# Block comparisons with the turns innermost, a chunk in three more steps, and a fourteenth shared pair ahead of the routed ones

## The chip, the core and the metric

The kernel runs on one core of a Trainium2 chip. The metric is device time in microseconds (us). Three runs of the kernel before took 564.23, 564.28 and 566.93 us; the median is 564.28 us. A run that was profiled took 563.65 us.

## The reference, cut to what matters

The input `x` holds 8 batches of 512 rows of 128 numbers. It is normalised, and causal attention with 16 heads of 8 dimensions and a mixture of experts both read the normalised rows. Their sum is added to `x`.

```
x = L0_attn_x
xn = _layernorm(x, axis=-1)
x = x + _L0_attn_ref(xn, ...) + _L0_ffn_ref(xn, ...)

# _L0_ffn_ref, over T = 4096 rows
shared = _ffn(xf, shared_gate, shared_up, shared_down)     # silu(x @ gw.T) * (x @ uw.T) @ dw.T
probs = jax.nn.softmax(xf @ gate_w.T, axis=-1)
topw, topi = jax.lax.top_k(probs, TOP_K)                   # 2 of 8 experts
topw = topw / (topw.sum(-1, keepdims=True) + 1e-20)
# routed: every row adds its two experts' _ffn, weighted
return (shared + routed).reshape(B, S, H)
```

All experts have 352 hidden units.

## The kernel before, in words

**Attention.** The unit of the loop is a step: scores of two of a group's four heads against some of the keys. A group has five steps (`TILES`: wide, wide, mixed, mixed, half), and with 8 batches of 4 groups there are 160 steps, 0 to 159. In a step PE makes the scores (`fill`, tile scT, L339), ACT takes their exponential (pT, L467), and PE later multiplies pT with the values (`attend`, tile av, L491). Nine steps ahead of that (`AHEAD`) a second set of scores is made (tile sc, L383), whose row maxima DVE takes (`maxima`: diag L417, tops L412, L421 and L422); PE turns the maxima (mT_ps, L439), and SP writes them into the rows of qs (L451), from which the later scores take them.

**Experts beside it.** The rows are worked on in pairs of blocks (256 rows). A pair is three chunks, one for each third of the hidden units. `chunk` multiplies on PE (tile gu, L653), takes a tanh on ACT (L658) and multiplies twice on DVE (th L659, h L661). When a pair's hidden units are there, `down` multiplies once for each of the two blocks (tile y, L684). A shared pair's y is added to `x_sb` by DVE (L695); a routed block's y is scaled by ACT (L691) and scattered by POOL's indirect DMA to `results` in HBM (L668). The list `stream` holds the order: `FIRST` = 13 shared pairs, then 36 routed pairs, then the other three shared pairs. The generator `experts` gives one chunk each time that `extra` is called. It is called before and between the first steps, and then once in each step of the main loop that isn't in the set `alone`: `set(range(3, 21, 2)) | {12, 16, 20}`, so steps 3, 5, 7, 9, 11, 12, 13, 15, 16, 17, 19 and 20 have no chunk. The first routed chunk comes in step 35, the last in step 142, and the last chunk of all in step 151.

**Routing.** `route` is a generator too, and goes on a little in each step. Near its end it finds which row stands at which place of the 72 blocks. Each of 64 turns (32 tiles of 128 rows, two choices) has a block number in `blk` and a position in `pos`. In each of steps 12 to 19 `compare(m)` takes eight turns (`PIECE`): one DVE operation compares all 72 block numbers with the eight (tile what, L1060), and eight DVE operations compare the positions (tile there, L1067). A step later ACT multiplies the comparison with the partition's number into the second half of what (L1074), and another step later `gather_up` makes eight matmuls of 144 columns (tile sums_of, L1079), which DVE adds to found (L1083). In step 20 and 21 DVE also finds the expert of each block (L1091, L1098).

**The end.** When all 72 routed blocks are scattered, POOL issues 16 DMAs that add `results` to `x_sb` (`gather`, L719), for two choices of eight batches. Batches 0 to 5 go first; those of batches 6 and 7, whose rows the last shared pairs still change, are put out after the last chunk. The list gives the batches' order; POOL's own order is the scheduler's. DVE adds the attention's projection (L584), for the last batch behind its adds from POOL, and SP writes the output (L1286) when a batch is complete.

**What sets the order.** The order on PE, DVE, ACT and SP is that in which the Python code issues (`manual_schedule`): in a step the scores, the look ahead, the chunk, the routing's piece, up to two waiting `down`s, then the values. Each of these engines works through its own list in this order. POOL's order is made by the scheduler. Tiles with one buffer (scT, sc) make a step's scores wait for the reader of those before, and gu, y, sums_of and other short tiles share three buffers of PSUM.

Of the kernel before, what the change touches and what calls it, by code (L numbers as in the profile page):

```python
# [10 lines left out]
F32 = mybir.dt.float32  # L11
I32 = mybir.dt.int32
BF16 = mybir.dt.bfloat16
# [12 lines left out]
P = 128  # L26
# [3 lines left out]
NT = B * NC  # L30
# [6 lines left out]
NE = 8  # L37
# [4 lines left out]
NP = TOPK * NT * P  # L42
BLK = P
MB = 2
FIRST = 13
LAST = (13, 14, 15)
PAIR = MB * BLK

# [1 line left out]
NB = (NP // BLK + NE - 1 + MB - 1) // MB * MB  # L50
# [3 lines left out]
PIECE = 8  # L54
# [13 lines left out]
def attn_moe_kernel(  # L68
# [14 lines left out]
    nc = tc.nc  # L83
# [44 lines left out]
    for i in range(NV):  # L128
        t = const.tile([P, NC, H, 32], F32, name=f"v_ext{i}")
# [11 lines left out]
    def constant_rows(t, rows):  # L141
# [11 lines left out]
        base=0, channel_multiplier=1,  # L153
# [14 lines left out]
    for t in v_ext:  # L168
# [10 lines left out]
        base=0, channel_multiplier=-1,  # L179
# [8 lines left out]
        base=0, channel_multiplier=0,  # L188
# [12 lines left out]
    for i in range(2):  # L201
        t = const.tile([P, NF, PAIR], F32, name=f"h{i}")
# [6 lines left out]
        own_p, pattern=[[0, 1]], base=0, channel_multiplier=1, allow_small_or_imprecise_dtypes=True  # L209
# [3 lines left out]
        upto_p, pattern=[[1, P]], base=0, channel_multiplier=0, allow_small_or_imprecise_dtypes=True  # L213
# [24 lines left out]
    def misc(shape, name, dtype=F32):  # L238
        return mi_ps.tile(shape, dtype, tag="mi", name=name)
# [347 lines left out]
    shared = [j for j in range(NT // MB) if j not in LAST] + list(LAST)  # L587
    stream = [("shared", j) for j in shared[:FIRST]]
    stream += [("routed", j) for j in range(NB // MB)]
    stream += [("shared", j) for j in shared[FIRST:]]  # L590
    weights, held, turned, scales = {}, {}, {}, {}
# [188 lines left out]
    hot_pool = early.enter_context(tc.tile_pool(name="hot", bufs=3))  # L780
    ro = early.enter_context(tc.tile_pool(name="router", bufs=1))
# [2 lines left out]
    count = ro.tile([P, PURE + 2 * MIXED], F32, name="count")  # L784
    count16 = ro.tile([P, NB], BF16, name="count16")
    nc.gpsimd.tensor_copy(count16, count_i)
    nc.gpsimd.tensor_copy(count[:, :PURE], count_i[:, : PURE * MB : MB])
    for i in range(2):
        nc.gpsimd.tensor_copy(count[:, ds(PURE + i * MIXED, MIXED)], count_i[:, PURE * MB :])
# [116 lines left out]
    def route():  # L906
# [5 lines left out]
        nc.vector.tensor_reduce(lmax, logits, AX.X, ALU.max)  # L912
        prob = ro.tile([P, NT, NE], F32, name="prob")
        hots = ro.tile([P, TOPK, NT, NE], F32, name="hots")
        equal = ro.tile([P, NT, NE], F32, name="equal")
        nth = ro.tile([P, NT, NE], F32, name="nth")
        left, tops = logits, [lmax]
        for i in range(TOPK):
            if i:
# [47 lines left out]
        nc.vector.reciprocal(psum, psum)  # L967
        total = ro.tile([P, NE], F32, name="total")
        nc.vector.tensor_copy(total, total_ps)
        placed_in = ro.tile([P, NT, NE], F32, name="placed_in")  # L970
        nc.scalar.copy(placed_in, place)
        yield

# [1 line left out]
        over = ro.tile([P, NE, most], F32, tag="rest", name="over")  # L975
# [24 lines left out]
        nc.vector.tensor_tensor(starts, ends, own, ALU.subtract)  # L1000
        apart = ro.tile([P, NE], F32, name="apart")
        paired = ro.tile([P, NE], F32, name="paired")
        where = ro.tile([P, NT, NE], F32, name="where")

        def every(v):
            return v.unsqueeze(1).to_broadcast([P, NT, NE])
# [34 lines left out]
        blk = ro.tile([P, TOPK * NT], BF16, name="blk")  # L1041
# [9 lines left out]
        whats, theres = {}, {}  # L1051

        def compare(m):
            these = ts(m, PIECE)

            def over(v):
                return v[:, these].unsqueeze(2).to_broadcast([P, PIECE, NB])

            what = hot_pool.tile([P, 2, PIECE, NB], BF16, name="what")
            nc.vector.tensor_tensor(  # L1060
                what[:, 0], count16.unsqueeze(1).to_broadcast([P, PIECE, NB]), over(blk),
                ALU.is_equal,
            )
            there = hot_pool.tile([P, PIECE, P], BF16, name="there")
            for t in range(PIECE):
                turn_ = m * PIECE + t
                nc.vector.tensor_scalar(  # L1067
                    there[:, t], upto_p, pos[:, ds(turn_, 1)], float(turn_ + 1),
                    ALU.is_equal, ALU.mult,
                )  # L1070
            whats[m], theres[m] = what, there
# [4 lines left out]
        def gather_up(m):  # L1076
            sums_of = misc([P, 2, NB], "sums_of")
            for t in range(PIECE):
                nc.tensor.matmul(  # L1079
                    sums_of, lhsT=theres[m][:, t], rhs=whats[m][:, :, t], start=(t == 0),  # L1080
                    stop=(t == PIECE - 1),
                )
            nc.vector.tensor_tensor(found, found, sums_of, ALU.add)  # L1083
# [25 lines left out]
        for m in range(pieces + 2):  # L1109
            if m >= 2:  # L1110
                gather_up(m - 2)
            if 1 <= m <= pieces:
                own(m - 1)
            if m < pieces:
                if m % 2 == 0:
                    two = PIECE // NC
                    nc.sync.dma_start(
                        to_table[:, ts(m // 2, two)],
                        rows[:, ts(m // 2, PIECE)].rearrange("p (b c) e -> p b c e", c=NC),
                    )  # L1120
                compare(m)
            else:
                experts_of[m - pieces]()
            yield
# [25 lines left out]
        nc.vector.tensor_scalar(token, number, -float(P), 0.0, ALU.add, ALU.max)  # L1150

    routing = route()
    done_routing = []

# [54 lines left out]
        due(first + (1 if b < 3 else 2), partial(project_qk, b, 1), behind_all)  # L1209
        due(at_ + (8 if b > 1 else 3), partial(project_v, b), behind_all)  # L1210
    routed = -2
    alone = set(range(3, 21, 2)) | {12, 16, 20}
    for t in range(AHEAD):
        while puts:
            puts.pop(0)()
# [131 lines left out]
```

## Time and profile before

| | |
|---|---|
| median of three runs | 564.28 us |
| the profiled execution | 563.65 us |
| its span | 561.5 us |
| PE busy | 530.3 us, 94% |
| DVE busy | 434.9 us, 77% |
| ACT busy | 354.0 us, 63% |
| POOL busy | 261.8 us, 47% |
| comparisons (sums_of, L1079) | 64 matmuls, first at 99.5, last at 127.8 us |
| comparisons (what, L1060) | 8 operations, 748 ns each, 93.1 to 119.7 us |
| first and last start of the adds from `results` (L719) | 523.5 and 552.0 us |

The span is the time between the first and the last instruction on the core; the execution's own time lies 2.15 us above it. A group of the profile gives a source line, an engine, the tile written and those read, the shape, how often it ran, its busy time in total and the mean of one in ns, and behind the second bar the engine's idle time before it and what ended that. A timeline gives the start in us, the time that the merged instructions took and, in brackets, the wait before them. The table of stretches gives the busy time of each engine in it, then the granted TensorE clock as a share of full speed, the busy share of the DMA engines and the GB/s that they moved. PE's matmuls overlap in a pipeline, so what one costs is read from start to start.

### The profile page before, as it was taken

The numbers are of one execution on the slowest core, as the hardware profiler recorded it, in microseconds if no ns is written. First come the engines' busy times: TensorE is split into PE (matmuls) and PEld (weight loads), VectorE is DVE, ScalarE is ACT, GpSimd is POOL, SyncE is SP. The second block draws the span as 40 slices with busy tenths as digits, with TensorE's granted clock in tenths as the row PEclk, the third lists the DMA queues.
The fourth block names the chain that finished last, engine by engine and source line by source line (L and its number), as shares of the span: only waits on it lengthen the run. The fifth ranks groups of instructions, "written<-read, shape, count | busy, mean of one in ns | idle before, by whom it ended". The sixth has DMA issues, their size and how long they took to land.

```text
span 561.5 us, 12501 instructions
## 1 busy us (share of the span) xinstructions
PE 530.3 (94%) x4495; PEld 380.2 (68%) x4495; DVE 434.9 (77%) x1057; ACT 354.0 (63%) x567; POOL 261.8 (47%) x442
## 2 busy tenths in 40 slices
PE   4899988899999999999999999999999999999994
PEld 2676655557675777677776777667776776778762
DVE  5878999999877777877787787778787877877741
ACT  4453444553566766777677776767677766766653
POOL 8630020001342656666556556656655756543630
PEclk9999999989999999999999999999999999999999
DMA  7651353625228583585639585675919586650694
GB/s 216 146 73 24 77 78 97 96 78 103 65 57 130 147 158 107 139 204 129 130 88 154 160 166 138 126 160 137 164 46 198 167 141 200 138 146 4 99 255 100
DMA packets 34114, 70.72 MB, mean 126 GB/s; under 512 B 7028, under 2 KB 9336, under 8 KB 34054
## 3 DMA queue, kind: packets, MB, share of 16 engines
q1 hardware_dynamic: 26278, 56.47, 44.4%
q0 software_dynamic: 6912, 13.20, 12.3%
q8 instruction: 36, 0.59, 0.5%
q10 hardware_dynamic: 864, 0.27, 0.2%
q14 instruction: 24, 0.20, 0.2%
HBM read 52.38 MB, written 17.33 MB: 124 GB/s over the span
## 4 chain that ended last, share of the span: by engine, by line
PE 76%; DVE 17%; ACT 2%; issue 2%; DMA 1%; POOL 0%; DVEq 0%; ACTq 0%
PE gu L653 24%; PE av L491 12%; PE y L684 11%; PE scT L339 9%; PE sc L383 9%; DVE diag L417 3%; PE qk_ps L264 3%; DVE tops L421 2%; DVE there L1067 2%; DVE th L659 1%; DVE h L661 1%; PE s_ps L629 1%; PE ot L542 1%; PE p_ps L579 1%; DVE stats L808 1%
## 5 line engine op out<-in xcount | busy, mean ns | idle before, releaser
L467 ACT ACTIVATE pT<-scT 128x1024 f32<-128x1024 f32 x156 | 159.9, 1025 | 62.3 <-PE scT L339 28.3
L474 POOL TENSOR_SCALAR_AFFINE_SELECT pT<-pT 128x256 f32<-128x256 f32 (+1 forms) x174 | 73.7, 437 | 185.3 <-ACT pT L467 182.3
L653 PE MATMUL gu<-sT,w 128*128 128x256 f32 (+1 forms) x480 | 122.7, 382 | 0.7 <-DMA w<-in_w_exp_dram 0.4
L417 DVE TENSOR_REDUCE diag<-sc 128x8 f32<-128x1024 f32 x64 | 78.2, 1222 | 44.1 <-PE sc L383 37.8
L658 ACT ACTIVATE th<-gu 128x256 f32<-128x256 f32 x156 | 59.8, 383 | 66.8 <-PE gu L653 62.7
L383 PE MATMUL sc<-ks,qs 33*128 33x128 f32 (+3 forms) x896 | 82.0, 283 | 10.3 <-DVE tops L422 4.4
L653 PEld LDWEIGHTS gu<-sT,w 128*128 128x128 f32 x480 | 76.7, 189 | 17.8 <-DMA w<-in_w_exp_dram 0.6
L491 PE MATMUL av<-pT,v_ext 128*32 128x512 f32 (+3 forms) x1024 | 83.4, 443 | 1.8 <-ACT pT L467 1.3
L659 DVE SCALAR_TENSOR_TENSOR th<-th,gu 128x256 f32<-128x256 f32 x156 | 65.0, 417 | 23.1 <-ACT th L658 18.6
L668 POOL DMA_INDIRECT results<-o,goal x72 | 73.2, 1016 | 16.3 <-issue 16.3
L615 POOL DMA_INDIRECT s<-table,token x72 | 69.9, 971 | 21.0 <-issue 16.0
L339 PE MATMUL scT<-qs,ks 35*128 35x512 f32 (+3 forms) x498 | 78.2, 371 | 1.2 <-ACT pT L467 1.2
L383 PEld LDWEIGHTS sc<-ks,qs 33*128 33x128 f32 (+1 forms) x896 | 66.5, 187 | 18.8 <-DVE diag L417 4.9
L339 PEld LDWEIGHTS scT<-qs,ks 35*128 35x128 f32 x498 | 39.4, 184 | 56.8 <-issue 24.5
L661 DVE TENSOR_TENSOR h<-gu,th 128x256 f32<-128x256 f32 x156 | 66.0, 423 | 5.4
L421 DVE TENSOR_REDUCE tops<-sc 128x2 f32<-128x768 f32 x64 | 60.8, 950 | 2.5 <-PE sc L383 1.8
L684 PE MATMUL y<-w,h 128*128 128x128 f32 x432 | 60.0, 275 | 0.6 <-DVE parts L266 0.6
L684 PEld LDWEIGHTS y<-w,h 128*128 128x128 f32 x432 | 57.2, 191 | 4.5 <-DVE parts L266 1.0
L371 ACT CAST sc<-mask_q 128x1024 f32<-128x1024 bf16 x50 | 50.9, 1019 | 6.1 <-DVE tops L422 4.5
L653 PE MATMUL gu<-xnT,ws_sb 128*128 128x256 f32 x192 | 54.2, 407 | 0.5 <-DVE v_ext L289 0.5
L491 PEld LDWEIGHTS av<-pT,v_ext 128*32 128x32 f32 x1024 | 25.7, 110 | 23.6 <-issue 14.4
L653 PEld LDWEIGHTS gu<-xnT,ws_sb 128*128 128x128 f32 x192 | 33.2, 192 | 11.7 <-issue 4.0
(209 smaller groups left out, 580.3 us busy)
## 6 DMA issues: line engine op xcount, KB each, us to landing
w<-in_w_exp_dram SPq DMA_DIRECT2D x40, 576.0 KB
ks<-dk SPq DMA_DIRECT2D x60, 128.0 KB
dq<-parts SPq DMA_DIRECT2D x16, 256.0 KB
dk<-parts SPq DMA_DIRECT2D x16, 256.0 KB
qs<-dq SPq DMA_DIRECT2D x64, 64.0 KB
x_sb<-results POOLq DMA_DIRECT2D x16, 256.0 KB
qs<-dq SPq DMA_DIRECT2D x30, 128.0 KB
table<-rows SPq DMA_DIRECT2D x4, 520.0 KB
```

Source lines behind the costliest of these rows:

```text
L339: nc.tensor.matmul(out_, lhsT=k[:, ts(i, P)], rhs=q[:, i * P :], start=first, stop=True, skip_group_check=True,)
L383: nc.tensor.matmul(ps[:, jj % 2, ts(at_, P) if count == 1 else ds(at_ * P, count * P)], lhsT=q[:, ts(c, P)], rhs=k[:, key * P : (key + cou ...
L417: nc.vector.tensor_reduce(diag[:, :, i // 2, :], ps.rearrange("p t (b k) -> p t b k", k=P), AX.X, ALU.max)
L421: nc.vector.tensor_reduce(tops[:, :, i // 2, 3], ps[:, :, : 3 * P], AX.X, ALU.max)
L467: nc.scalar.activation(pT, ps, AF.Exp, scale=D**-0.5)
L474: m = nc.gpsimd.affine_select(out=d, in_=d, pattern=[[0, d.shape[1]], [1, P]], compare_op=ALU.is_ge, fill=0.0, base=0, channel_multiplier=-1,)
L491: nc.tensor.matmul(av[32 * jj : 32 * jj + 32, c * P :], lhsT=v_ext[b % NV][:, c, at_, :], rhs=weights, start=(c == 0 and g % 2 == 0), stop ...
L653: nc.tensor.matmul(gu[:, i, part], lhsT=w[c][:, ds(i * FP + f * P, P)], rhs=sT[:, part], start=True, stop=True,)
L659: nc.vector.scalar_tensor_tensor(th, th, 1.0, gu[:, 0], ALU.add, ALU.mult)
L661: nc.vector.tensor_tensor(h[own_, f], gu[own_, 1], th[own_], ALU.mult)
L668: d = nc.gpsimd.indirect_dma_start(results, bass.IndirectOffsetOnAxis(ap=goal[:, at_ : at_ + 1], axis=0), o, None, bounds_check=PLACES - 1 ...
L684: nc.tensor.matmul(y, lhsT=h[:, f, ts(c, P)], rhs=w[c % len(w)][:, ds(2 * FP + f * P, P)], start=(f == 0), stop=(f == NF - 1),)
```

## The change

Three things change.

First, the comparison tile `what` is laid out with the eight turns innermost: 72 blocks of eight turns in place of eight turns of 72 blocks. A new constant `every_block`, made by POOL's iota while the kernel starts, holds each block's number eight times, so that both inputs of the comparison run with step 1 innermost. The matmul of a turn now reads every eighth element of what as its moving operand: its 144 columns stand 16 bytes apart, where they were contiguous. The values are the same.

Second, `alone` loses steps 12, 16 and 20, so these get a chunk. And `FIRST` is 14, so the pair with number 13 comes ahead of the routed pairs. Together these leave the routed chunks at their steps 35 to 142, and the last chunk moves from step 151 to step 148. The order of the instructions on PE, DVE and ACT differs from before only in that the three chunks and two `down`s stand among the comparisons and no longer in steps 149 to 152; SP's order is the same, and POOL's has the iota more.

Third, four tiles of the router share two buffers by their tags (equal and where, nth and placed_in).

```diff
-FIRST = 13
+FIRST = 14
 LAST = (13, 14, 15)
...
+    every_block = ro.tile([P, NB, PIECE], BF16, name="every_block")
+    nc.gpsimd.iota(
+        every_block, pattern=[[1, NB], [0, PIECE]], base=0, channel_multiplier=0,
+        allow_small_or_imprecise_dtypes=True,
+    )
...
-        equal = ro.tile([P, NT, NE], F32, name="equal")
-        nth = ro.tile([P, NT, NE], F32, name="nth")
+        equal = ro.tile([P, NT, NE], F32, tag="equal", name="equal")
+        nth = ro.tile([P, NT, NE], F32, tag="nth", name="nth")
...
-        placed_in = ro.tile([P, NT, NE], F32, name="placed_in")
+        placed_in = ro.tile([P, NT, NE], F32, tag="nth", name="placed_in")
...
-        where = ro.tile([P, NT, NE], F32, name="where")
+        where = ro.tile([P, NT, NE], F32, tag="equal", name="where")
...
-            def over(v):
-                return v[:, these].unsqueeze(2).to_broadcast([P, PIECE, NB])
-
-            what = hot_pool.tile([P, 2, PIECE, NB], BF16, name="what")
+            what = hot_pool.tile([P, 2, NB, PIECE], BF16, name="what")
             nc.vector.tensor_tensor(
-                what[:, 0], count16.unsqueeze(1).to_broadcast([P, PIECE, NB]), over(blk),
+                what[:, 0], every_block, blk[:, these].unsqueeze(1).to_broadcast([P, NB, PIECE]),
                 ALU.is_equal,
             )
...
-                    sums_of, lhsT=theres[m][:, t], rhs=whats[m][:, :, t], start=(t == 0),
+                    sums_of, lhsT=theres[m][:, t], rhs=whats[m][:, :, :, t], start=(t == 0),
...
-    alone = set(range(3, 21, 2)) | {12, 16, 20}
+    alone = set(range(3, 21, 2))
```

## The prediction, made before the changed kernel ran

> **What bounds the kernel now.** I read the page first (which engine is full), then the stretch that the change touches, then the end. Times below are microseconds after the start of the span, unless a duration is meant.
>
> ```profile
> PE 530.3 (94%) x4495; PEld 380.2 (68%) x4495; DVE 434.9 (77%) x1057; ACT 354.0 (63%) x567; POOL 261.8 (47%) x442
> PE 76%; DVE 17%; ACT 2%; issue 2%; DMA 1%; POOL 0%; DVEq 0%; ACTq 0%
> ```
>
> PE carries the kernel: 94% busy and 76% of the chain that ended last. So work moved from one PE-bound place to another moves no time; it must go where PE waits, or leave a place where nothing else holds the end. Both ends of this move therefore have to be looked at. The steps of the comparisons (steps 12 to 21 of the attention loop; step 12 begins with the mixed scores at 90.27, step 22 with those at 129.75) are the place where DVE leads instead. The busy time by stretch, of that stage and of its two slow spots:
>
> ```profile
> core 0: us, PE busy (x) PEld busy (x) DVE busy (x) ACT busy (x) POOL busy (x), PEclk, DMA share, GB/s
> 90.27:129.75 39.48, 33.13 (x330) 20.47 (x330) 38.04 (x124) 19.72 (x25) 0.00 (x0) 0.91 0.48 108
> 97.20:100.65 3.45, 3.45 (x17) 2.46 (x18) 3.41 (x12) 0.86 (x2) 0.00 (x0) 0.51 1.03 152
> 121.10:124.55 3.45, 3.45 (x26) 1.35 (x18) 3.35 (x12) 0.83 (x2) 0.00 (x0) 0.51 0.21 47
> ```
>
> DVE is busy 38.04 of 39.48, PE 33.13: PE waits 6.35 there. In two pieces of about 3.41 the granted clock was 0.51, so PE also lost 3.4 of full-speed work. The groups that the change alters, and two that price what no row shows directly (group: busy total, mean ns of one):
>
> ```profile
> L1067 DVE TENSOR_SCALAR there<-upto_p,pos 128x128 bf16<-128x128 bf16 x64 | 11.1, 244 | 0.0
> ...
> L253 ACT COPY ordered<-xnT 128x512 f32<-128x512 f32 x7 | 7.8, 1108 | 0.0
> ...
> L1060 DVE TENSOR_TENSOR what<-count,blk 128x576 bf16<-128x576 bf16 x8 | 6.0, 748 | 0.0
> ...
> L1079 PE MATMUL sums_of<-what,there 128*128 128x144 bf16 x64 | 5.9, 240 | 0.0
> ...
> L872 ACT COPY xnT<-tp 128x512 f32<-128x512 f32 x7 | 4.1, 581 | 2.7 <-PE tp L871 2.5
> ```
>
> A matmul's mean includes its pipeline, so its price is read from starts. PE's timeline has eight sums_of from 101.50 to the next at 102.10, and three matmuls of the placement:
>
> ```profile
> 69.24 0.59 PE L958 MATMUL place<-run,ones 128*128 128x256 bf16 x1
> 69.65 0.61 PE L961 MATMUL place<-both,before 128*128 128x256 bf16 x1
> 70.08 0.19 PE L964 MATMUL place<-run,ones 128*128 128x8 bf16 x1
> 101.50 0.67 PE L1079 MATMUL sums_of<-what,there 128*128 128x144 bf16 x8
> ```
>
> Eight contiguous sums cost 0.60. The placement reads its moving operand with a step of 64 bytes between elements, and 256 columns took 0.41 and 0.43: 1.64 ns a column against 0.52 for sums_of with its weight loads.
>
> The end: POOL's timeline of the adds of the routed results (L719), and DMA by stretch (last three columns: clock, share, GB/s).
>
> ```profile
> 536.54 1.75 POOL L719 DMA_DIRECT2D x_sb<-results  x2 [0.41 <-DMA x_sb<-results]
> 545.53 1.75 POOL L719 DMA_DIRECT2D x_sb<-results  x2 [7.24 <-DMA x_sb<-results]
> 551.97 0.86 POOL L719 DMA_DIRECT2D x_sb<-results  x1 [4.69 <-DMA x_sb<-results]
> 533.00:543.00 10.00, 9.96 (x96) 6.58 (x95) 6.01 (x18) 4.39 (x6) 3.48 (x4) 1.00 1.13 204
> 543.00:552.50 9.50, 7.52 (x120) 4.21 (x116) 0.00 (x0) 6.74 (x7) 2.28 (x3) 1.00 0.92 262
> 555.50:556.00 0.50, 0.00 (x0) 0.00 (x0) 0.36 (x3) 0.34 (x1) 0.00 (x0) 1.00 0.29 49
> 556.00:556.50 0.50, 0.41 (x2) 0.20 (x2) 0.00 (x0) 0.01 (x1) 0.00 (x0) 1.00 0.00 0
> ```
>
> PE is full up to 543, but the DMA engines are full too (share about 1), with a second chain of their own: each add waits for the one before. The last moves data until 556.0, and the final DVE add (L584, at 557.66) waits for it as well as for PE.
>
> **The change, part by part.**
>
> *The iota on POOL.* POOL's IOTA of 128 columns took 0.23, its 2,048-column MEMSET 1.81 (0.85 ns a column), so 576 columns cost 0.5 to 0.7. It sits in POOL's queue ahead of the router's constants and of the first statistics (L829 before), and POOL waited 1.62 for DVE there at 15.13. Cost 0; without that wait it would delay the third batch's rows by 0.7.
>
> *The shared buffers* (placed_in with nth, where with equal) add waits for the readers of the old contents. The last of these, the second choice's hots, ran on DVE before the placement matmuls, and placed_in and where come behind those. Cost 0.
>
> *The eight comparisons on DVE.* 748 ns for 576 elements, 424 for the 256-element f32 h: 1.01 ns an element. If packed pairs halve the elements, 288 of them cost 457 by that slope, a gain of 0.29 each and 2.3 in all; the other bound is no gain. I take the gain: all three operands are now two bytes wide with step 1 innermost, and the 128-column bf16 L1067 at 244 already lies under the slope's 295. [...]
>
> *Three chunks into steps 12, 16 and 20.* DVE gets three pairs th and h (0.77 from start to start, 115.17 to 115.94) and the pair's two x_sb updates at 0.20: 2.7, against the 2.3 saved. DVE stays level (+0.4). PE gets three times gu at 1.06 and twelve y records at 1.57: +4.75. Behind gu in PE's queue stand sums_of and the attention sums; behind th in DVE's stand found and the next comparison.
>
> *sums_of with a step.* Its moving operand now has its 144 columns 16 bytes apart. No row has this step. Low bound: unchanged, 0. High bound: the placement's 1.64 ns, 144 x 1.64 = 0.236 each, 1.89 for eight, +1.29 a piece, +10.3 for eight pieces. Between lies gu's price, contiguous four-byte columns: 1.06 for four of 256 is 1.04 ns, 0.15 each, +0.6 a piece, +4.8. I take the high bound: it is the only stepped two-byte moving operand here, and 16 bytes are not free elsewhere: the ACT copy L253, which writes four-byte elements 16 bytes apart, took 1108 ns where L872 took 581. [...]
>
> *What of it lies beside other work.* Added on PE: 4.75 + 10.3 = 15.05. Room: waits 6.35 plus 3.4 if the clock stays full once PE no longer pauses; less 1.37 of step 13 (waits of 0.28 and 1.09 in PE's timeline), where PE has nothing added and still waits for DVE. Room 8.4, so the stage grows by 15.05 - 8.4 = **6.65** and turns PE-bound. The rest of the loop up to the last routed pair has the same work at the same steps, so everything shifts.
>
> *The tail.* The shared pair leaves steps 149 to 152: 4.75 of PE work. One gu of 1.06 (537.62) covered ACT's output copy and exp, which the next scores wait for until 538.80 anyhow; it becomes a wait. PE would finish 3.7 earlier. But DMA does not: from the pair at 545.53 each add still waits for the one before, and the last moves data until 556.0. From the DMA's rows the DVE add could start perhaps 0.6 after that, at 556.6, so at most 1.1 is gained. On the other side, SP sends the first six outputs (541.69) behind the last shift's rows, which PE now releases some 3.6 earlier. In before those outputs filled the DMA's pause between two adds; earlier they share the engines with adds that are still running. DMA moved 406 GB/s from 545 to 547, so an output of 256 KB takes 0.65; if four are crowded in ahead of an add, it is late by 2.6. Bounds -1.1 to +2.6; I take **0**, as the two mechanisms oppose each other and neither has a row.
>
> *Sum.* The profiled execution took 563.65 (span 561.5). 563.65 + 6.65 + 0 = 570.3. That execution lies 0.63 under the median of the runs, so on the median's scale **570.9**, 1.2% slower.
>
> **The rivals.** A difference under 0.5% (2.8 us: 561.5 to 567.1) can't be told from none.
>
> *A, the forecast:* the stepped operand costs about four times, 570.9.
>
> *B, the step costs half of that.* 4.8 + 4.75 = 9.5 of added PE work against 8.4 of room, +1.1, DVE's +0.4 beside it, and about 0.5 because two full engines wait for each other: 566.3. [...] Against: the placement's rows.
>
> *C, faster.* The step is free and the last adds land earlier than I read: the stage grows by DVE's 0.4 alone and the end follows PE, -3.7: 561.0. It needs both, and decides as soon as sums_of stays under about 0.07 us a matmul and the final DVE add waits for PE alone. For it: PE is on the chain nearly to the end (p_ps at 556.91). Against: the DMA is busy until 556.0, and the add waits for that.
>
> *D, the move is hidden twice.* The step is free, DMA holds the end: +0.4 and 0, 564.7.
>
> *E, the clock.* As A, but the 0.5 clock comes again in the stage: +3.4, 574.3. For it: it came twice in before. Against: PE waited there before each time.
>
> **How the numbers follow.** A 0.50, B 0.20, D 0.13, C 0.09, E 0.08. The predicted time is A's, 570.9. C lies below 561.5, which gives faster 0.09. D and two thirds of B give same 0.26, the rest slower 0.65. The range leaves out C and the outer end of E: from 563.6 (D with the tail's -1.1) to 575.0 (A with the tail's worst and 1.4 of waits for shared accumulators). A's own range, with the tail's bounds and one more or less of room, is 568.8 to 574.6.
>
> **What the changed profile would show.** L1081 (sums_of): eight in about 1.9 from start to start, mean near 410 ns; 0.60 speaks for C or D, about 1.2 for B. L1062 (what): near 457 ns; 748 says that the packed mode did not come, and DVE then adds 2.3. PE's waits in the comparison stage fall from 6.35 to under 2, DVE's busy share falls, and the stage (12th to 22nd step) grows from 39.5 to about 46. The granted clock there stays 1.00. The end: no gu after step 148, PE's waits grow by about 3.7 after the routed pairs, the three late adds still end the wait of L584's line, and the outputs start some 3.6 earlier against the adds. I am wrong if the stage shrinks, if the step is free, or if L584 still waits for PE alone at a time 3.7 nearer.

## The result, and the profile after

The changed kernel took 578.64 us (median of six runs, 573.90 to 584.68) against 563.85 us for the kernel before (six runs on the same chip, 562.39 to 566.93). The ratio is 1.0251, with a 95% interval from 1.0223 to 1.0280: 2.5% slower. Ratios here and below leave out runs that took over 1.5% more than the fastest of the same kernel, which differ from the others by a lower granted clock (here the run of 584.68, with 0.963). The forecast was 570.9 with a range that ended at 575.0, so the direction was right and the size was not. The profiled execution took 577.4 us, with a span of 575.6.

From two landmarks in PE's timeline (the first fills of steps 12 and 22) and one in POOL's (the last scatter of routed rows, after which nothing but the adds, shared pairs and the last attention block is left), the two spans divide like this:

| part of the span | before | after | difference |
|---|---|---|---|
| start to step 12 | 90.27 | 90.13 | -0.14 |
| steps 12 to 21, the comparisons | 39.48 | 51.00 | +11.52 |
| step 22 to the last scatter | 391.05 | 390.76 | -0.29 |
| last scatter to the end | 40.68 | 43.71 | +3.03 |
| span | 561.48 | 575.60 | +14.12 |

Where nothing was edited, nothing moved. The comparisons lost 11.5 us, and the end, from which work was taken away, lost 3 as well.

The page of the changed kernel, busy time by engine and the chain of work that ended last:

```profile
PE 545.1 (95%) x4495; PEld 385.5 (67%) x4495; DVE 433.3 (75%) x1057; ACT 354.3 (62%) x567; POOL 263.2 (46%) x443
...
PE 75%; DVE 12%; DMA 4%; issue 3%; POOL 3%; ACT 2%; SPq 0%; POOLq 0%; DVEq 0%; ACTq 0%
```

PE is busy 14.8 us longer with the same 4495 matmuls; DVE has 1.6 less. In the chain DVE fell from 17% to 12%, and DMA rose from 1% to 4%. Of DMA's share, one transfer of 8.27 us lies at the end and is new on the path (shown below). Its longest piece, 11.04 us at 246.47, lies in the middle part, which took no longer than before, so the chain's shares alone do not tell where the time went. The busy time by stretch, of the whole stage and of a piece in it (columns: length, busy time and count by engine, granted clock, DMA share, GB/s):

```profile
90.13:141.13 51.00, 49.47 (x355) 28.19 (x356) 39.04 (x130) 20.60 (x28) 0.00 (x0) 0.87 0.37 84
97.58:111.23 13.65, 13.52 (x74) 7.81 (x74) 9.68 (x39) 3.04 (x5) 0.00 (x0) 0.50 0.72 106
```

PE now has no room: 49.47 busy of 51.00. DVE is busy 39.04 and idle 12. And for 13.65 us without a break PE ran at half clock, where before there were two pieces of 3.41. The groups that the change altered (busy total, mean ns of one, idle before):

```profile
L1081 PE MATMUL sums_of<-what,there 128*128 128x144 bf16 x64 | 17.7, 433 | 0.0
...
L1069 DVE TENSOR_SCALAR there<-upto_p,pos 128x128 bf16<-128x128 bf16 x64 | 11.1, 247 | 0.0
...
L1062 DVE TENSOR_TENSOR what<-every_block,blk 128x576 bf16<-128x576 bf16 x8 | 3.6, 450 | 0.0
...
L1085 DVE TENSOR_TENSOR found<-found,sums_of 128x144 f32<-128x144 f32 x8 | 2.4, 304 | 3.6 <-PE sums_of L1081 3.6
...
L788 POOL IOTA every_block<- 128x576 bf16 x1 | 1.1, 1133 | 0.0
```

The comparison `what` fell from 748 to 450 ns, 2.4 us in all. The sums rose from a mean of 240 to 433 ns, and DVE's add into found, which never waited before, now waits 3.6 us for them. PE's timeline of the changed kernel, two groups of eight sums, the first at half clock and the second at full:

```profile
100.30 2.23 PE L1081 MATMUL sums_of<-what,there 128*128 128x144 bf16 x8
...
116.92 2.21 PE L1081 MATMUL sums_of<-what,there 128*128 128x144 bf16 x8
```

Eight took 0.67 in this view before, at full clock. From start to start within a group one takes 0.253 to 0.257 us, in groups at half clock as in groups at full. In the profile of before it is 0.063 at full clock and 0.120 in the one group at half clock. So what limits the stepped sums is not PE's clock.

The end of the chain of work, the changed kernel:

```profile
544.85 1.43 PE av L491 x24
548.09 8.27 DMA qs<-mT
557.42 2.72 PE av L491 x24
```

And PE's timeline at the same place; the brackets are the wait before, and what ended it:

```profile
551.14 0.40 PE L324 MATMUL scT<-mask_k,eye 64*128 64x128 bf16 x8
554.93 0.73 PE L339 MATMUL sc<-qs,ks 35*128 35x512 f32 x1 [3.40 <-DMA qs<-mT]
556.40 0.79 PE L339 MATMUL sc<-qs,ks 35*128 35x512 f32 x1 [0.73 <-DMA qs<-mT]
```

The last shift's rows (qs<-mT, 8 KB each, put by SP at L451) are on the path for 8.27 us: the second of them, issued at 548.09, landed at 556.35. In before the same fill waited for ACT alone:

```profile
544.58 0.59 PE L339 MATMUL sc<-qs,ks 35*128 35x512 f32 x2 [0.65 <-ACT pT L467]
```

Directly after that wait PE's clock was halved again, for 6.83 us in the middle of the last attention sums. The busy time by stretch of the changed kernel, from the issue of the rows to the end of the wait, and of the piece at half clock (columns as above):

```profile
547.40:554.90 7.50, 3.52 (x48) 2.11 (x48) 0.84 (x3) 3.52 (x4) 1.36 (x2) 1.00 1.12 216
554.96:561.79 6.83, 6.10 (x48) 2.95 (x48) 0.00 (x0) 1.60 (x2) 1.76 (x2) 0.50 0.95 269
```

While the rows were under way the DMA engines were full (share 1.12).

Three explanations had to be told apart. *The stepped operand*: the reads of sums_of at 16 bytes a column make the loss. *The move*: three chunks cost in the comparison stage more than they save at the end. *The clock*: the longer half-clock piece is an accident of this execution. The experiments ran on another chip, where the kernel before took 558.4 to 559.9 us; the part between step 22 and the last scatter took 385.5 to 389.6 there instead of 391 (398.2 in e7, whose edit falls into it). So ratios are compared, and stages between profiles of that chip. The kernel before was not profiled there: where one of its stages is set beside that of an experiment, the chips differ.

### The profile page after: what moved, and what is told of

Read it like the earlier page. It is cut to its first block, busy times and chain, and to the rows that moved or that the text cites. A ratio compares the mean times of both kernels' runs of the same rounds, so it can differ in the third digit from the quotient of the medians.

```text
span 575.6 us, 12502 instructions
## 1 busy us (share of the span) xinstructions
PE 545.1 (95%) x4495; PEld 385.5 (67%) x4495; DVE 433.3 (75%) x1057; ACT 354.3 (62%) x567; POOL 263.2 (46%) x443
## 4 chain that ended last, share of the span: by engine, by line
PE 75%; DVE 12%; DMA 4%; issue 3%; POOL 3%; ACT 2%; SPq 0%; POOLq 0%; DVEq 0%; ACTq 0%
PE gu L653 23%; PE av L491 11%; PE y L684 10%; PE scT L339 9%; PE sc L383 9%; PE sums_of L1081 3%; PE qk_ps L264 2%; DVE diag L417 2%; DMA results<-o,goal 2%; DMA qs<-mT 1%; DVE tops L421 1%; DVE th L659 1%; PE s_ps L629 1%; DVE h L661 1%; PE p_ps L579 1%
## 5 line engine op out<-in xcount | busy, mean ns | idle before, releaser
L491 PE MATMUL av<-pT,v_ext 128*32 128x512 f32 (+3 forms) x1024 | 84.9, 450 | 1.4 <-ACT pT L467 0.9
```

Source lines behind the costliest of these rows:

```text
L491: nc.tensor.matmul(av[32 * jj : 32 * jj + 32, c * P :], lhsT=v_ext[b % NV][:, c, at_, :], rhs=weights, start=(c == 0 and g % 2 == 0), stop ...
```

## Experiments

All with the kernel before beside them. "Stage" is steps 12 to 21, with the half-clock time in it; "to p_ps" and "to end" count from the last scatter to PE's last output projection and to the end of the span. Stages and ends are those of the one profiled execution, ratios those of the timed runs.

| kernel | ratio to before, 95% | stage (at half clock) | to p_ps | to end |
|---|---|---|---|---|
| before (first chip) | 1 | 39.48 (6.83) | 37.27 | 40.68 |
| changed (first chip) | 1.0251 (1.0223 to 1.0280) | 51.00 (13.65) | 39.98 | 43.71 |
| e1, layout alone | 1.0225 (1.0148 to 1.0301) | 49.92 (20.48) | 38.08 | 41.79 |
| e2, move alone | 1.0173 (1.0095 to 1.0251) | 42.72 (6.83) | 40.51 | 43.91 |
| e3, layout in pairs, no move | 0.9955 (0.9925 to 0.9985) | 35.76 (3.41) | 39.94 | 43.66 |
| e4, changed, no adds | one run, 565.87 us | 46.75 (0) | 34.61 | 38.01 |
| e5, layout in pairs and move | 1.0113 (1.0072 to 1.0153) | 41.75 (3.41) | 40.35 | 44.07 |
| e6, as e5, a hold on the adds | 1.0111 (1.0061 to 1.0161) | 43.14 (10.24) | 37.21 | 46.02 |
| e7, see below | 1.0169 (1.0107 to 1.0231) | 36.21 (3.41) | 33.12 | 42.81 |
| e3b, layout in fours, no move | one run, 560.48 us | 36.25 (3.41) | 38.90 | 42.61 |
| e9, as e3, move turned round | 0.9962 (0.9931 to 0.9994) | 35.70 (8.67) | 41.36 | 45.09 |
| e10, changed again | 1.0205 (1.0107 to 1.0303) | 60.10 (40.96) | 40.22 | 44.26 |

**The two parts, one at a time.** e1 keeps the new layout and puts the chunks back:

```diff
-FIRST = 14
+FIRST = 13
...
-    alone = set(range(3, 21, 2))
+    alone = set(range(3, 21, 2)) | {12, 16, 20}
```

> The layout alone (turns innermost, every_block, stepped sums_of), with 13 shared pairs first and the chunks where they were. Theory: the stepped operand is the main loss. Eight sums_of take 2.05 us instead of 0.60 whatever the clock, +11.6 on PE; PE waited 6.35 in the comparison stage and keeps about 1.5 of that, so the stage grows from 39.5 by 6.7 to about 46; the way from the last scatter to the end stays 40.7. Total about 570.5, ratio 1.012. [...] Rival: the added chunks, not the step, made the stage grow; then the stage stays at 39 to 40 and the ratio is 0.995 to 1.002.

Measured 570.96 us, 1.0225: nearly twice the loss expected, and nearly that of the whole change. The sums again took 0.253 to 0.257 us from start to start.

e2 keeps the old layout and makes the move alone (the two lines of e1 in the other direction, on the kernel before):

> The move alone (14 shared pairs first, chunks in steps 12, 16 and 20), with the old layout. Theory: DVE, which was busy 38.0 of 39.5 us in the stage, gets 2.7 more, so the stage grows by 2.7 to 3.5; at the end the last shift's rows are sent earlier into DMA engines that are full of adds and still land about when those are done, PE waits about 4 us for them, the clock falls, and the way from the last scatter to the end grows from 40.7 to about 43.7. Total about 570, ratio 1.010 to 1.012. Rival for the end: the late landing came from the shift of the whole program against the DMA, not from the move; then the way to the end is 37 to 40.7 and the ratio 0.999 to 1.006.

Measured 568.26 us, 1.0173. So each part alone makes the kernel slower, and together they do not add up: 12.6 and 9.7 us by these ratios against 14. The likely reason is that the sums take up the very waits of PE that the chunks were meant to fill. Both parts also came with more half clock: the mean granted clock of the timed runs was 0.972 to 0.976 in e1 and 0.967 to 0.986 in e2, against 0.983 to 0.997 of the kernel before in the runs that were compared.

**Is it the step?** e3 keeps the layout idea but puts only two turns innermost, so that the columns of a turn stand 4 bytes apart; the chunks are where they were before:

```diff
-    every_block = ro.tile([P, NB, PIECE], BF16, name="every_block")
+    every_block = ro.tile([P, NB, 2], BF16, name="every_block")
...
-            what = hot_pool.tile([P, 2, NB, PIECE], BF16, name="what")
+            what = hot_pool.tile([P, 2, PIECE // 2, NB, 2], BF16, name="what")
...
-                what[:, 0], every_block, blk[:, these].unsqueeze(1).to_broadcast([P, NB, PIECE]),
+                what[:, 0], every_block.unsqueeze(1).to_broadcast([P, PIECE // 2, NB, 2]),
+                blk[:, these].rearrange("p (a g) -> p a g", g=2).unsqueeze(2).to_broadcast(
+                    [P, PIECE // 2, NB, 2]
+                ),
...
-                    sums_of, lhsT=theres[m][:, t], rhs=whats[m][:, :, :, t], start=(t == 0),
+                    sums_of, lhsT=theres[m][:, t], rhs=whats[m][:, :, t // 2, :, t % 2], start=(t == 0),
```

> As the layout alone, but with two turns innermost: the comparison still has step 1 on all operands, and the matmul's columns stand 4 bytes apart instead of 16. [...] Rival (any step other than 1 costs the full price): eight sums_of stay at 2.05, ratio 1.012.

It took 556.6 us, 0.9955 (0.9925 to 0.9985), and has the lowest ratio of the kernels here, with e9's next to it. Its PE timeline, one group of eight sums at half clock and one at full:

```profile
100.31 1.17 PE L1084 MATMUL sums_of<-what,there 128*128 128x144 bf16 x8
...
102.61 0.69 PE L1084 MATMUL sums_of<-what,there 128*128 128x144 bf16 x8
```

Its groups of the sums and the comparison:

```profile
L1084 PE MATMUL sums_of<-what,there 128*128 128x144 bf16 x64 | 6.0, 239 | 0.0
...
L1062 DVE TENSOR_TENSOR what<-every_block,blk 128x576 bf16<-128x576 bf16 x8 | 3.6, 448 | 0.0
```

And its comparison stage, busy time by engine:

```profile
91.66:127.42 35.76, 31.46 (x330) 19.94 (x330) 35.38 (x124) 19.64 (x25) 0.00 (x0) 0.95 0.51 115
```

The comparison is as cheap as in the changed kernel (448 ns), and the sums cost nearly what they cost before: 0.065 to 0.067 from start to start, and now the clock does matter to them (1.17 for eight at half clock, 0.69 at full). The stage is 35.76, and DVE is busy in 35.38 of it: it is DVE's stage, so what the packed comparison saves DVE can shorten it. It is 3.7 shorter than the kernel before's on the first chip, of which the comparisons explain 2.4; it also had 3.41 us less at half clock.

e3b puts four turns innermost, a step of 8 bytes, with the 2s of e3's layout turned into 4s (and `t // 4`, `t % 4` in the matmul):

> Four turns innermost: the moving operand of sums_of steps by 8 bytes. [...] Time 555 to 562 us.

Its PE timeline, two groups of eight sums, the first at half clock and the second at full:

```profile
98.65 1.22 PE L1084 MATMUL sums_of<-what,there 128*128 128x144 bf16 x8
...
101.26 1.20 PE L1084 MATMUL sums_of<-what,there 128*128 128x144 bf16 x8
```

Hardly a difference again, as at 16 bytes. One took 0.127 from start to start (0.131 at half clock). So for 144 columns at full clock: 0.063 us at a step of 2 bytes, 0.066 at 4, 0.127 at 8, 0.253 at 16. From 4 to 16 bytes the time grew with the address range of the 144 columns: 576 bytes in 0.066, 1152 in 0.127 and 2304 in 0.253 are 8.7, 9.1 and 9.1 bytes a nanosecond. The placement in the profile of before, with 64 bytes between columns, took 1.64 ns a column, no more than the 1.76 at 16 bytes. Why the time goes this way with the step was not shown. The doubled price of the sums hardly shows in e3b's stage (36.25 against 35.76), since it fits beside DVE.

**Does the move pay when the sums are cheap?** e5 is e3 with `FIRST` 14 and steps 12, 16 and 20 taken out of `alone`, as in the change:

> Pairs innermost (step of 4 bytes in sums_of) together with the move (FIRST 14, chunks in steps 12, 16, 20). Theory 1 (the last shift's rows queue in the DMA behind the adds): the stage from step 12 to step 22 takes 1 to 2 us more than with the pairs alone, since 4.75 us of PE work meet some 3.7 us of waits that are left; the rows are issued 15.5 us after the last scatter, land 7 to 8 us later, PE waits 3 us and more in step 155, and from the last scatter to the end it is 42 to 44 us. Ratio to the kernel before 0.996 to 1.003. Rival (the end follows PE once sums_of is cheap): 37 to 38 us from the last scatter to the end, ratio 0.988 to 0.992.

Measured 564.67 us, 1.0113, worse than either theory. Against e3 the two ratios differ by 1.6%, some 9 us. The two profiles differ by 4.8 (spans of 562.79 and 557.95), as e3's profiled run took 559.71 us, 3.1 above its median. The stage of e5's profile by engine:

```profile
89.78:131.53 41.75, 36.16 (x354) 23.40 (x355) 38.48 (x132) 20.34 (x28) 0.00 (x0) 0.96 0.45 102
```

The three chunks bring PE 4.70 (36.16 less 31.46) and DVE 3.10 (38.48 less 35.38), and the stage grows by 5.99. DVE had 0.38 idle in e3; it has 3.27 in e5, because now the two engines wait for each other, PE at y for DVE's h (2.4 us in two waits, against 0.8 in one), ACT and DVE for PE's scores. PE's waits in e3's stage (4.3) looked like room, but they were waits for DVE, and a chunk is work for DVE too. The end did not pay it back (44.07 against 43.66): PE's timeline shows the changed kernel's wait once more.

```profile
541.57 0.76 PE L339 MATMUL sc<-qs,ks 35*128 35x512 f32 x1 [3.20 <-DMA qs<-mT]
```

e9 moves the pair in the other direction, on e3: `FIRST` 12 and {10, 14, 18} added to `alone`.

> Pairs innermost, but the shared pair is moved the other way: FIRST 12, so that steps 10, 14 and 18 get no chunk either and four pairs instead of three come last. Theory 1 (a chunk in the comparison stage costs its PE time and something more, because the stage's waits are for DVE, which the chunk loads too; at the end PE now has no cover): the stage and with it the first scatter come 5 to 6 us earlier than with pairs alone, from the last scatter to the output projection PE needs 3.5 us more (41 to 42), to the end 44 to 45, no wait over 1 us for the last shift's rows; ratio to the kernel before 0.990 to 0.996. Rival (the waits only grow when chunks leave, since DVE paces the comparisons): the stage shortens by under 2 us, ratio 0.997 to 1.005.

556.76 us, 0.9962 (0.9931 to 0.9994): between the two theories' ranges, and not to be told from e3's 0.9955. The end went as theory 1 had it (41.36 to the output projection, 45.09 to the end, no wait for the rows). The stage did not get shorter, 35.70 against 35.76, with 8.67 of half clock in it against 3.41; how much it would gain at the same clock was not measured. The split of e3, which is that of the kernel before, is not beaten in either direction.

**Why did the end not get nearer?** The end varies between profiles, and also without the move it was longer on this chip than the 40.68 of before: 41.79 (e1), 42.61 (e3b), 43.66 (e3). With the move it was 43.91 (e2), 44.07 (e5) and 44.26 (e10). So the move's price at the end, 3.03 in the two profiles of the first chip, is between 0.3 and 2.5 by those of the second. PE's waits for the last shift's rows tell the two kinds apart better: none in e1, 1.10 in e3 and 1.11 in e3b, but 3.03 (e2), 3.93 (e5) and 4.62 (e10) with the move, each in two waits.

e4 is the changed kernel without the sixteen adds of `gather`, so the routed experts' part is missing from its output:

```diff
-        with on_pool():
-            d = nc.gpsimd.dma_start(
-                x_sb[:, ts(b, NC), :],
-                results[ts(i * B + b, S)].rearrange("(p c) e -> p c e", c=NC),
-                accum_op=ALU.add,
-            )
-        for o in placed:
-            tc.add_manual_dep(d.ins, o.name, SYNC, reason="any block may hold these tokens")
+        return
```

> The changed kernel without the 16 DMAs that add the routed results to the rows, so the routed experts' part is missing from the output. Theory: the last shift's rows land in 2 to 3 us instead of 8, PE does not wait for them, the clock stays full at the end, and the way from the last scatter (POOL) to the end of p_ps is 33 to 34 us; it was 36.8 in the kernel before and 40.0 in the changed one. Rival (the rows are late for another reason, such as SP's queue): the wait of about 4 us and the 40 stay.

As expected at the end: PE was done 34.61 after the last scatter, 5.4 earlier than in the changed kernel and 2.7 earlier than in the kernel before, and the fill that waited 3.40 for the rows now waits for ACT:

```profile
546.43 0.50 PE L339 MATMUL sc<-qs,ks 35*128 35x512 f32 x2 [0.65 <-ACT pT L467]
```

So PE's part of the gain is there, and the adds' transfers take it. The timing is plain in the traces. With the pair gone SP issues the last rows 15.5 and 16.2 us after the last scatter instead of 19.4 and 20.1. The thirteenth add is issued at 15.65 in the changed kernel and at 16.28 before. The rows used to come 3 us after the group of thirteen; now they come on top of it. Issued 3.9 us earlier, they landed no earlier: 22.9 and 24.5 us after the last scatter in the changed kernel, 23.6 and 23.8 in the kernel before. In e4, without the adds, each landed 1.9 us after its issue.

e6 is e5 with the ninth add of the Python list made to wait until the last rows have landed:

```diff
+HELD = 8
...
+            if n == B * NG - 1:
+                last_rows.append(d.ins)
...
+        if len(to_gather) == HELD - 1:
+            for o in last_rows:
+                tc.add_manual_dep(d.ins, o.name, SYNC, reason="the last rows go first")
...
-                    if to_gather and (to_gather[0][1] < kept or through):
+                    if to_gather and (to_gather[0][1] < kept or through) and (
+                        len(to_gather) > HELD or last_rows
+                    ):
```

> As the kernel with pairs innermost and the move, but the ninth of the sixteen adds (and so all after it) waits for the last shift's rows. Theory 1: the rows land within 4 us of their issue, PE waits under 1 us in step 155, the granted clock stays full there, PE reaches the output projection 34.6 us after the last scatter (as without the adds) and the end comes 38 to 39 us after it; ratio to the kernel before 0.988 to 0.993. Rival (the adds, held back, set the end instead): PE is as early, but the last DVE add waits for the adds, 41 to 44 us, ratio 0.996 to 1.003.

In the trace the hold did not bind. POOL's timeline of the adds:

```profile
533.30 0.87 POOL L723 DMA_DIRECT2D x_sb<-results  x1 [1.41 <-DMA x_sb<-results]
535.93 0.87 POOL L723 DMA_DIRECT2D x_sb<-results  x1 [1.76 <-DMA x_sb<-results]
537.18 0.87 POOL L723 DMA_DIRECT2D x_sb<-results  x1 [0.39 <-DMA x_sb<-results]
538.66 1.76 POOL L723 DMA_DIRECT2D x_sb<-results  x2 [0.61 <-DMA x_sb<-results]
547.61 1.76 POOL L723 DMA_DIRECT2D x_sb<-results  x2 [7.19 <-DMA x_sb<-results]
554.01 1.76 POOL L723 DMA_DIRECT2D x_sb<-results  x2 [4.64 <-DMA x_sb<-results]
```

POOL's ninth add went out at 535.93, before the rows were issued (536.72 and 537.38). POOL's order is the scheduler's, and by its semaphores the add that waits for the rows stands fifteenth there, at 554.01, when they had long landed (542.78). So e6 did not test what was written for it. What differed from e5 is POOL's order, with twelve adds and not thirteen ahead of the long pause, and that the first add came 4.34 us after the last scatter instead of 2.75. PE waited 0.69 for ACT and only 0.83 for the rows and was earlier than in e5 (37.21 against 40.35, not the 34.6 expected: 3.41 us of half clock followed all the same), but the end came later, 46.02, outside the ranges of the theory and of its rival. As the rival had it, DVE's timeline shows the last add of the output waiting for an add of `gather` instead of PE:

```profile
558.17 0.76 DVE L588 TENSOR_TENSOR x_sb<-p_ps,x_sb 128x256 f32<-128x256 f32 x2 [2.55 <-DMA x_sb<-results]
```

e7 was meant to be the same hold without the move. The kernel that ran also had `FIRST` at 14, with steps 12, 16 and 20 still without a chunk: the pair goes ahead of the routed ones, and the routed chunks come three steps later. So it does not test what was written for it:

> Pairs innermost without the move, the ninth add waiting for the last shift's rows. Theory 1: here the rows are issued 19.4 us after the last scatter, when the first thirteen adds have nearly drained; holding them back keeps PE's wait in step 155 at 0.65, no clock drop follows, 40.5 to 41 us from the last scatter to the end, ratio 0.991 to 0.995. Rival (the 43.7 us of the one profile with pairs alone had nothing to do with the adds): 43 to 44 again, or the same spread. Rival (the held adds set the end): above 44.

The hold did not bind here either: the add that waits for the rows is the fourteenth on POOL, issued at 549.67, and they had landed at 541.92. SP issued them 9.25 us after the last scatter, amid the adds, and PE waited 3.20 and 0.73 for them.

The kernel shows something else. The last scatter came 10 us later than in e3 (524.33 against 514.28), PE had only 33.12 us left after it, and still the end came at 42.81. DVE's timeline:

```profile
562.13 0.76 DVE L588 TENSOR_TENSOR x_sb<-p_ps,x_sb 128x256 f32<-128x256 f32 x2 [6.86 <-DMA x_sb<-results]
```

The last output add began 37.0 us after the last scatter in e6 and 37.8 in e7, both times when the adds let it. In the kernel before it began 36.9 after the scatter, when PE let it:

```profile
557.66 0.87 DVE L584 TENSOR_TENSOR x_sb<-p_ps,x_sb 128x256 f32<-128x256 f32 x2 [1.77 <-PE p_ps L579]
```

There the adds moved data until 556.0, 35.2 after the scatter. So by that profile an earlier PE could bring the end at most some 1.7 us nearer while the adds are there (36.9 less 35.2, an estimate), and only if its rows do not meet them.

**The clock.** e10 is the changed kernel once more:

> The changed kernel once more, unedited, beside the same runs of the kernel before. Theory: ratio 1.022 to 1.030; sums_of again 0.256 us from start to start; the granted clock is again halved near 97 us, but for another number of 3.41-us stretches than the four of the first trace (one to four), and the stage from step 12 to step 22 is 46 us plus half of what lies at half clock in it. If the drop is fixed by the program, it is four stretches again and 51 us.

The ratio, 1.0205 (1.0107 to 1.0303), is that of the runs of 568.43, 571.85 and 576.06 us, and its theory had 1.022 to 1.030. Two more took 582.25 and 659.60 us, the latter at a mean granted clock of 0.749. The profiled execution is the one of 582.25 and had 40.96 us of half clock in the stage, twelve stretches of 3.41 and not one to four; the sums kept their 0.253 to 0.257 there. The half-clock time is not fixed by the program. With e4 this makes a scale for one and the same stage. The busy time by engine in e4's stage:

```profile
90.41:137.16 46.75, 45.23 (x354) 25.61 (x354) 38.75 (x130) 20.61 (x28) 0.00 (x0) 1.00 0.41 92
```

That is e4, whose code before the adds is that of the changed kernel: no half clock, 46.75. The changed kernel: 13.65 at half clock, 51.00, which is 4.25 or 0.31 us for each. e10's profile, of a run 2.4% above that kernel's fastest: 40.96 and 60.10, 0.33 for each, where the theory had half. The timed runs of the changed kernel agree: from a mean granted clock of 0.989 to one of 0.973 the span grew from 572.1 to 578.5 us and the half-clock time from 12.6 to 31.2 (an estimate, twice the missing share of the clock times the span), 0.34 for each. It is under the 0.5 that a wholly clock-bound PE would lose, as the stepped sums do not slow down (0.253 to 0.257 at either clock). Of the 11.52 us by which the stage grew, 4.25 are thus half clock.

What turns the clock down was not settled. At the end of the kernel there is a pattern. In the changed kernel, e5, e7, e10, e2, e6 and e3, in which PE waited 4.13, 3.93, 3.93, 4.62, 3.03, 0.83 and 1.10 us for the last rows, a half-clock piece of 3.41 to 10.24 us began during the wait or within 0.6 us of its end. In before, e1, e4 and e9, which did not wait for them, there was none before the last transposes. e3b waited 1.11 and kept its clock that long too. In the comparison stage the clock went down between 96.5 and 99.7 us in nine of twelve profiles, during PE's wait of 0.8 to 1.3 us in step 13 or within 0.9 us of its end; e4 and e5 had that wait (0.94 and 0.95) and no drop there. Busy time shows another pattern. Of the 42 drops in the twelve profiles, 39 followed a stretch of 3.41 us in which PE was busy 2.52 us or less. The other three (114.08 and 131.15 in e1, 132.76 in e10) followed stretches in which PE was busy throughout, with stepped sums in each. But such a stretch is not enough: one with 1.85 us busy, up to 502.46 in e5, was followed by full clock. The half-clock time in the stage was 3.41 us or a multiple of it in every profile but e4's (none) and e9's (8.67). How busy PE was before a drop differs: in the changed kernel it was busy for 0.03 of the 3.41 us before the drop at 554.96, but for 2.31 of those before the drop in the stage, with a longest wait of 0.94, and for 13.52 of the 13.65 us at half clock.

## Why the prediction was wrong

*The step price was the right term, and a little too small.* "144 x 1.64 = 0.236 each, 1.89 for eight" measured 0.256 each by the same reckoning and 2.05 from the first group's start to the next matmul's (100.30 to 102.35), against 0.60; eight groups make +11.6 instead of +10.3. Taking the high bound from the placement's rows was right. e1, e3 and e3b show it to be the step: with the same comparison (450, 448 and 449 ns), the price follows the step alone. At 16 bytes one took 0.253 us, at 8 bytes 0.127, at 4 bytes 0.066 and at 2 bytes, without a step, 0.063: eight elements cost four times the price, four twice, two hardly more. No run shows the free step that C and D take for this operand.

*The layout's gain was right:* what at 450 ns for a forecast 457. That packed pairs halve the elements was the author's assumption; no run shows the halving itself, only the times: 748 ns before, 450 after, 448 in e3.

*The stage without the clock was right.* 39.48 + 6.65 = 46.1 forecast; e4, with the clock full, 46.75.

*First failed step: "plus 3.4 if the clock stays full once PE no longer pauses".* The room of 8.4 counted the two half-clock pieces as something that a busier PE would be spared. The stage kept and lengthened them: PE's waits did fall from 6.35 to about 1.5, and the clock was halved for 13.65 us in place of 6.83. That is 4.25 us of stage, against e4. Why the clock fell as it did stays open. It was rival E (574.3, chance 0.08), which priced 3.4 for it, and that rival was nearest to the result.

*Second failed step: the tail at 0, "bounds -1.1 to +2.6".* It measured +3.03 on the first chip; on the second, where the end was longer without the move too, single profiles put the move's price lower. The place was read rightly in part: PE's 3.7 us are not gained since DMA holds the end. e4 shows PE done earlier once the adds are gone (34.61 us after the last scatter against 39.98), and in e6 and e7 the last output add waits for the adds (2.55 and 6.86 us). But the price was looked for at the outputs crowding the adds. The transfers that collided were the 8 KB of rows that PE waits for, now issued 3.9 us earlier and on top of thirteen adds (7.4 and 8.3 us to land, against 1.9 in e4). The move's own effect on SP ("behind the last shift's rows, which PE now releases some 3.6 earlier") was in the text, as the moment when outputs follow, and its other half, that the rows themselves now meet the adds, was not drawn.

*A step that is only half proven:* the forecast let the chunks fill PE's waits in the stage. In the changed kernel the waits are gone because the stepped sums fill them. With cheap sums they are not filled (e5: +5.99 for 4.70 of PE work), so rivals C and D, 561.0 and 564.7 with a free step, would have been wrong too: e5's ratio of 1.0113 on 563.65 is some 570.

*Small ones:* the iota took 1.13 us, not 0.5 to 0.7, and stayed hidden (step 10 began at 84.13, before at 84.28). Added up against the profiled execution: 570.3 forecast, stage +4.87, end +3.03, the unchanged parts -0.43, and 0.37 less around the span make 577.4.

## What to carry to other kernels

A layout that helps one engine is read by another: before packing elements for DVE, look at the step with which PE will read the result, and put innermost only as many as keep PE's columns within 4 bytes (here two of two bytes: 448 ns for DVE's comparison against 748, and 450 with eight; and 0.066 us a matmul on PE against 0.063). An engine's waits are room for moved work only if that work does not also load the engine that it waits for (in e5 the stage grew by 5.99 us for 4.70 of PE work). When work leaves the end of a kernel, look at what small transfer its engine issues next and what large ones that now meets: a gain on PE can come out as a longer wait for 8 KB (here 4.13 us).

## What the runs showed of the hardware that was not expected

- The moving operand of a matmul with 144 two-byte columns: 0.063 us from start to start at a step of 2 bytes, 0.066 at 4, 0.127 at 8, 0.253 at 16. The last is the same at half clock (2.23 for eight against 2.21), while the 4-byte step is not (1.17 against 0.69).
- DVE's comparison of 576 two-byte elements ran at 450 ns with runs of eight equal-step elements and at 448 with runs of only two: here the second level of the broadcast cost nothing.
- Two transfers of 8 KB, issued at the end of a group of thirteen adds of 256 KB, landed 7.4 and 8.3 us after their issue (changed kernel), and 1.9 us after it without the adds (e4). Issued 3 to 5 us after the thirteenth add they took 3.3 to 4.7 us, and PE waited at most 1.1 for them (before, e1, e3, e3b).
- The same program had 13.65 us of half clock in its comparison stage in one execution and 40.96 in another, in pieces that are multiples of 3.41; e4, with the same code up to there, had none. Of the 42 drops of the clock in the twelve profiles, 39 followed 3.41 us in which PE was busy 2.52 us or less; what turns the clock down was not shown.
